# Loading one of 98 quads of a gathered edge table by single-row transfers of SyncE

## The chip, the cores and the metric

The kernel runs on one core of a Trainium2 chip. The metric is the device time of one execution in microseconds. Before the change it was 1997.35 us, the median of three runs (1996.39 to 2000.05). Five engines work side by side, each through its own list of instructions in order: TensorE (PE in the profile, PEld for its weight loads), VectorE (DVE), ScalarE (ACT), GpSimd (POOL) and SyncE (SP), which here does nothing but issue transfers. They wait for each other by semaphores.

## The reference

A layer of a graph network with attention: 12500 nodes with 128 features, 200000 edges sorted by their target, four heads of 32.

```python
h = max(layernorm(x), 0) @ W_node.T               # per node, 4 heads x 32
e = edge_attr @ W_edge.T                          # per edge
att = sum(concat(h[src], h[tgt], e) * a, -1)      # per edge and head
att = where(att > 0, att, 0.2 * att)
m = maximum(segment_max(att, tgt), 0)
ex = exp(att - m[tgt])
denom = segment_sum(ex, tgt) + (num_edges - deg) * exp(-m)
out = x + segment_sum((ex / denom[tgt]) * h[src], tgt)
```

Each edge needs the row of its source node, and the sources are in no order.

## The kernel before

A first part computes for every node a row of 137 numbers (548 bytes) and writes these rows to a table in memory. It holds the node's values h, ones, and its share of the attention as a source. A narrower table, `side`, holds the share as a target.

The edges are then worked off in **groups** of 512 places (511 edges and one place for what is carried over), four groups to a **quad**. There are 392 groups and 98 quads, numbered 0 to 97. A chunk is 128 places, so a quad has 16 chunks, and its rows fill a tile `ga` of 128 partitions by 4 groups by 4 chunks by 137 numbers. Eight such places exist: quad q lies in place q mod 8. Up to four quads make a **super**, on which a softmax is computed at once.

For each quad the following is done, by the functions named:

- `gather` (line 181) has GpSimd fetch the rows by indirect transfers, one for a chunk: 128 rows by 128 row numbers that lie in `srci`. From quad 8 on each transfer raises one of eight semaphores, and `add_sources` has ScalarE wait for the count of its quad before it copies the attention shares out of `ga` into `U` (line 735).
- `fetch`, `fetch_windows`, `fetch_inputs`, `fetch_targets` collect SyncE's loads into lists, and `issue` (line 598) puts out the next of a list: `ea`, the edge features, two in a quad; `pw`, target shares, from a row number that a register holds; `db`, the edges' places among their nodes; `inputs`, rows of x for the residual; and the results' stores to `out`. The row numbers come by register loads (line 584), one for `pw` and one for `inputs` in a quad, of as many words as the quad has windows: one up to quad 35, two up to quad 74, four behind that. `dr` (line 643), the targets for the softmax, comes once in a super.
- `all_logits` compares places on VectorE (`targets`, into `at`) and multiplies on TensorE (`logits`, into `lg`). `ea` and `pw` of quad q+2 are issued in the logits of quad q, `db` of quad q+2 at the start of the logits of quad q+1, since it has two places.
- `softmax` works on a super, and `sums` multiplies the rows of `ga` by the weights and adds them up by target on TensorE (line 1122); a division follows and the store.

The program is written out in one order, and each engine gets its instructions in it. `together` interleaves the steps of several of these functions: the sums of a quad run beside the logits of a quad some four later, one group of the one beside one of the other. `sums` ends each group with `issue("inputs", "results")`. GpSimd's list is therefore nothing but gathers, and each waits only until the place of the quad eight before it is free, that is, until TensorE has finished that quad's sums.

The tile `db` has two places of 4 x 512 words. From quad 10 on the places of edges are single bytes, so that most of the tile is free.

Of the kernel before, what the change touches and what calls it, by code (L numbers as in the profile page):

```python
# [39 lines left out]
QUADS = 8  # L40
# [6 lines left out]
SQUARE = 32  # L47
TWO = 2
HELD = 3
SETS = max(NODE_T, QG * J)  # L50
PAD = 1 << 20

# [17 lines left out]
def kernel(  # L70
# [39 lines left out]
    nc = tc.nc  # L110
    NT = -(-(N + P) // P)
    NP = NT * P
# [8 lines left out]
    table = dram.tile([NP, ROW], F32, name="table")  # L121
# [33 lines left out]
    quads = blocks(G, QG)  # L155
# [10 lines left out]
    ga_all = consts.tile([P, QUADS, QG, J, ROW], F32, name="ga")  # L166
    GA, GATHERED = {}, set()
    arrived = [tc.alloc_semaphore(f"rows{k}") for k in range(QUADS)]
    landings = {}

    def gather(q, rows, width, lo, hi):

        g0, m = quads[q]
        ga = GA[q] = ga_all[:, q % QUADS]
        chunks = lambda i: -(-min(E - (g0 + i) * NE + 1, GE) // P)
        for i in range(lo, hi):
            if chunks(i) < J:
                nc.vector.memset(ga[:, i, chunks(i):, :], 0.0)
        order = [(i, j) for i in range(lo, hi) for j in range(chunks(i))]
        for i, j in order:  # L180
            came = nc.gpsimd.indirect_dma_start(  # L181
                out=ga[:, i, j, 0:width], out_offset=None, in_=rows,
                in_offset=bass.IndirectOffsetOnAxis(ap=srci[:, g0 + i, j:j + 1], axis=0))
            if q >= QUADS:
                came.then_inc(arrived[q % len(arrived)], 16)
                tc.no_tile_sem_insts.add(came.ins.name)
                tc.add_to_no_dep_group(f"rows{q}", came.ins)
                landings[q] = landings.get(q, 0) + 16
# [27 lines left out]
    with tc.manual_schedule():  # L216
# [165 lines left out]
        def fetch_targets(q):  # L382
            g0, m = quads[q]
            n = P if class_of(q)[1] == WIDE else NARROW
            db, rows = db_all[:, q % 2], dst.rearrange("(g e) -> g e", e=GE)
            if q >= OFFSETS:
                db = db.rearrange("p g e -> p (g e)")[:, 0:QG * GE // 4].bitcast(U8)
                db, rows = db.rearrange("p (g e) -> p g e", e=GE), offset
            DB[q] = db
            return [(db[:n, lo:lo + k, :],  # L390
                     rows[g0 + lo:g0 + lo + k].unsqueeze(0).to_broadcast([n, k, GE]))
                    for lo, k in blocks(m, QG if q >= OFFSETS else PLACES_BY)]
# [150 lines left out]
    with tc.tile_pool(name="work", bufs=2) as work, \  # L543
# [91 lines left out]
        def fetch_rows(s):  # L635
            g0, m = groups(s)
            dr = DR[s] = turned.tile([SBG * H, NE + 2], I32, name="dr", bufs=2)
            if finer(s) > 1:
# [4 lines left out]
            nc.sync.dma_start(dr[0:H * m, :],  # L643
                              dst_rows[g0:g0 + m, :].unsqueeze(0).to_broadcast([H, m, NE + 2]))

        def open_logits(q):
            if q == supers[of_quad[q]][0]:
                fetch_rows(of_quad[q])
            if q + 2 < nq:
                fetch(q + 2)  # L650
            AT[q] = work.tile([P, QG, GE], BF16, name="at")
# [68 lines left out]
        def add_sources(q):  # L720

            s = of_quad[q]
            g0, m = quads[q]
            s0, sm = groups(s)
            keep_logits(q)
            if s not in U:
                U[s] = turned.tile([P, J, SBG * H], F32, name="U", bufs=2)
            f = finer(s)
            u = U[s][:, 0:J // f, 0:sm * H * f].rearrange("p c (h w) -> p w c h", h=H)[
                :, (g0 - s0) * f:(g0 - s0 + m) * f]  # L730
            if q >= QUADS:
                nc.scalar.wait_ge(arrived[q % len(arrived)],
                                  sum(landings[a] for a in range(QUADS, q + 1)
                                      if a % len(arrived) == q % len(arrived)))
            taken = nc.scalar.copy(u, GA[q][:, :m].rearrange("p g (f c) r -> p (g f) c r", f=f)[  # L735
                :, :, :, R_SRC:R_SRC + H])
            if q >= QUADS:
                tc.declare_no_dep(taken.ins, group=f"rows{q}",
                                  reason="a semaphore counts the gathers of this quad")
                tc.declare_fence(taken.ins, group=f"rows{q}")  # L740
            for kept in (EA, DB, PW, AT):
                del kept[q]
# [318 lines left out]
        def sums(q):  # L1061
# [36 lines left out]
            for i in range(m):  # L1098
# [31 lines left out]
                if not later and i == (2 if k > 1 else 1):  # L1130
                    entered()
                    if k == 1:
                        settled()
                complete(new)
                if k == 1:
                    begun.append((q, i, ga, hot, pt, acc, fc))
                if i == 2 and QUADS <= q < first_fold - 5 and of_quad[q + 1] == s:
# [735 lines left out]
```

## Time and profile before

| What | Value |
|---|---|
| median of three runs | 1997.35 us |
| the profiled execution's own time | 1993.67 us |
| its span, first to last instruction | 1991.8 us |
| busy: GpSimd / VectorE / TensorE / ScalarE | 75% / 60% / 57% / 16% of the span |
| indirect gathers on GpSimd | 1494 from the table, 72 from x |
| mean busy share of the 16 DMA engines | 0.4 to 0.5 after the first part |
| software queue (GpSimd's) / hardware queue (SyncE's) | 109.61 MB / 116.14 MB |

The page counts GpSimd's indirect transfers as busy, but not what SyncE does to issue one: an issue appears with its duration only in the timeline and in the answers on one source line, as engine SPq. There a row gives the shortest, the median and the longest duration in ns and the first and last start in us. A row of the waits names the waiting line, whom it waited for, the total in us, how often and the longest.

### The profile page before, as it was taken

How to read it: one execution, taken by the hardware profiler on the slowest of the kernel's cores; microseconds unless marked ns; L12 is line 12 of the kernel's file. 1: busy time of each engine (PE TensorE's matmuls, PEld its weight loads, DVE VectorE, ACT ScalarE, POOL GpSimd, SP SyncE). 2: the span in 40 equal slices, each digit the busy share in tenths (PEclk: the TensorE clock that was granted, in tenths of full speed). 3: DMA queues.
4: the chain of work that ended last, by engine and by line, in shares of the span. 5: the costliest groups of instructions: out<-in, count | busy, mean ns of one | idle time of the engine just before them, and what ended most of it. 6: DMA issues, size and time to landing. Idle time of an engine off the chain costs nothing. (4 is left out here: it accounts for less than half of the span.)

```text
span 1991.8 us, 18871 instructions
## 1 busy us (share of the span) xinstructions
PE 1140.5 (57%) x5116; PEld 780.2 (39%) x5116; DVE 1193.3 (60%) x2615; ACT 318.3 (16%) x1077; POOL 1491.3 (75%) x1585
## 2 busy tenths in 40 slices
PE   6566676556464655554646555546465555455565
PEld 5444454334243433342434333334343333233344
DVE  8676786456374554564746546647465474367676
ACT  6564111001011010010110100101000011122122
POOL 7777777777777777777777777777777777777774
PEclk9788788676676776767767767677777666777778
DMA  7754754434344444344444444444444444444442
GB/s 254 209 141 98 175 132 111 105 93 110 97 108 104 119 98 114 96 108 112 119 101 113 106 110 108 108 114 115 104 107 105 105 120 98 112 109 116 99 106 51
DMA packets 167748, 229.57 MB, mean 115 GB/s; under 512 B 60827, under 2 KB 100669, under 8 KB 167638
## 3 DMA queue, kind: packets, MB, share of 16 engines
q0 software_dynamic: 50112, 109.61, 24.7%
q1 hardware_dynamic: 115824, 116.14, 20.5%
q10 hardware_dynamic: 1702, 2.59, 0.4%
q8 instruction: 41, 0.67, 0.1%
q14 instruction: 69, 0.57, 0.1%
HBM read 210.74 MB, written 17.43 MB: 115 GB/s over the span
## 5 line engine op out<-in xcount | busy, mean ns | idle before, releaser
L181 POOL DMA_INDIRECT ga<-table,srci x1494 | 1413.7, 946 | 456.0 <-issue 407.9
L1122 PE MATMUL acc<-ga,hot 128*113 128x137 f32 (+1 forms) x2928 | 546.2, 346 | 81.5 <-DVE hot L1031 53.6
L1122 PEld LDWEIGHTS acc<-ga,hot 128*113 128x113 f32 (+1 forms) x2928 | 486.5, 216 | 182.2 <-issue 100.4
L956 DVE SCALAR_TENSOR_TENSOR pt<-pt,spare,acc 1x133 f32<-1x133 f32 x113 | 38.3, 339 | 523.5 <-ACT den_of L950 522.1
L691 PE MATMUL lg<-at,pw 112*96 112x512 bf16 (+2 forms) x392 | 157.2, 438 | 278.7 <-DVE at L658 265.8
L688 PE MATMUL lg<-ea,by_pair 128*96 128x512 f32 (+1 forms) x392 | 229.6, 671 | 7.1 <-ACT tg L701 7.1
L658 DVE TENSOR_TENSOR at<-const_ps,db 112x1024 bf16<-112x1024 f32 (+1 forms) x176 | 212.8, 1210 | 3.3 <-DMA db<-offset 3.3
L1089 DVE TENSOR_TENSOR ga<-ga,ex_ps 128x1056 f32<-128x1056 f32 x147 | 182.2, 1239 | 0.0
L792 PE MATMUL t_ps<-ident,U 128*64 128x128 f32 (+2 forms) x210 | 47.2, 397 | 208.9 <-ACT U L735 208.9
L735 ACT COPY U<-ga 128x64 f32<-128x64 f32 x98 | 29.0, 297 | 806.5 <-DMA ga<-table,srci 806.5
L1091 DVE TENSOR_TENSOR hot<-const_ps,slot 128x896 f32<-128x896 f32 (+1 forms) x147 | 144.1, 980 | 0.0
L792 PEld LDWEIGHTS t_ps<-ident,U 128*64 128x64 f32 (+2 forms) x210 | 37.1, 201 | 234.9 <-ACT U L735 231.6
L887 PE MATMUL ex_ps<-ident,stack 128*128 128x128 f32 x105 | 28.6, 424 | 170.2 <-DVE stack L879 157.0
L975 PEld LDWEIGHTS acc<-pt,spare 1*2 1x2 f32 x226 | 14.1, 86 | 209.0 <-issue 200.8
L691 PEld LDWEIGHTS <-pw 112*96 112x96 bf16 (+2 forms) x392 | 54.4, 139 | 102.2 <-issue 99.1
L887 PEld LDWEIGHTS ex_ps<-ident,stack 128*128 128x128 f32 x105 | 18.5, 215 | 184.3 <-ACT stack L877 184.3
L1048 DVE TENSOR_TENSOR ga<-ga,ex_ps 128x528 f32<-128x528 f32 x92 | 63.6, 693 | 38.6 <-ACT xs L893 38.5
L181 POOL DMA_INDIRECT ga<-in_x_dram,srci x72 | 68.3, 948 | 23.2 <-issue 19.2
L701 ACT COPY tg<-lg 96x512 f32<-96x512 f32 (+1 forms) x51 | 29.5, 578 | 293.8 <-PE lg L691 284.4
L920 PE MATMUL acc<-ga,hot 128*81 128x137 f32 x176 | 43.2, 334 | 52.7 <-ACT ga L928 50.8
L717 PE MATMUL t_ps<-tg,of_head 96*64 96x512 f32 (+3 forms) x96 | 72.5, 848 | 0.0
L717 PEld LDWEIGHTS t_ps<-tg,of_head 96*64 96x64 f32 (+3 forms) x96 | 12.0, 174 | 154.1 <-issue 150.9
(209 smaller groups left out, 1318.6 us busy)
## 6 DMA issues: line engine op xcount, KB each, us to landing
ea<-in_edge_t_dram SPq DMA_DIRECT2D x196, 256.0 KB
ga<-table,srci POOLq DMA_INDIRECT x1494
db<-offset SPq DMA_DIRECT2D x53, 256.0 KB
db<-in_dst_dram SPq DMA_DIRECT2D x20, 320.0 KB
db<-offset SPq DMA_DIRECT2D x35, 160.0 KB
table<-row SPq DMA_DIRECT2D x9, 616.5 KB
xt<-in_x_dram SPq DMA_DIRECT2D x9, 576.0 KB
inputs<-in_x_dram SPq DMA_DIRECT2D x92, 56.0 KB
```

Source lines behind the costliest of these rows:

```text
L181: came = nc.gpsimd.indirect_dma_start(out=ga[:, i, j, 0:width], out_offset=None, in_=rows, in_offset=bass.IndirectOffsetOnAxis(ap=srci[:, ...
L658: nc.vector.tensor_tensor(AT[q][:span, i:i + n, :].rearrange("p g e -> p (g e)"), part_ps[:span].to_broadcast([span, n * GE]), DB[q][:span ...
L688: nc.tensor.matmul(lg, by_pair[:, begin:begin + n], ea[:, i // 2, :], start=half == 0 and i == 0, stop=False, skip_group_check=True)
L691: nc.tensor.matmul(lg, PW[q][:span, begin:begin + n], at[:span, i, :], start=False, stop=full and i == quads[q][1] - 1, skip_group_check=True)
L717: nc.tensor.matmul(TP[s][:groups(s)[1] * H], of_head[supers[s][1], p][:n], tg[:n], start=p == 0, stop=False, skip_group_check=True)
L792: nc.tensor.matmul(t_ps[:R, j * P:(j + 1) * P], u[:, j, :R], ident, start=False, stop=j == C - 1, skip_group_check=True)
L887: nc.tensor.transpose(turned_ps[:, j, :], stack[:, j * P:(j + 1) * P], ident)
L920: nc.tensor.matmul(acc, hot[:, i, 0, 0:acc.shape[0]], ga[:, i, 0, :], start=False, stop=stop)
L1048: engine.tensor_tensor(val, val, weight.unsqueeze(3).to_broadcast([P, J, H, HW]), op=OP.mult)
L1089: nc.vector.tensor_tensor(val, val, weight.unsqueeze(3).to_broadcast([P, TWO * J, H, HW]), op=OP.mult)
L1091: nc.vector.tensor_tensor(hot[:, i:i + TWO, :, 1:1 + span].rearrange("p g j c -> p (g j) c"), lane_ps[:, 0:span].unsqueeze(1).to_broadcast ...
L1122: nc.tensor.matmul(acc, hot[:, i, j, 0:1 + span], ga[:, i, j, :], start=new and j == J - 1 and not second, stop=k > 1 and i % k == k - 1 a ...
```

## The change

Quad 84, the 85th, is not gathered. Its 2048 rows come by 2048 transfers of SyncE, one row of 548 bytes each, into a place of their own in the free part of the tile `db`. Each takes its row number from a register. A register load fetches 16 such numbers at a time from one partition of the same tile; they come there by a small transfer of 128 numbers for a chunk, and VectorE multiplies them by 548 to make addresses in bytes. `single_rows` is called behind each group's sums, from quad 11 on, and issues eight rows, so that 256 calls make the 2048. It asks for the numbers of the next chunk ahead, at a chunk's first call. Two semaphores count the rows, and ScalarE waits for both ahead of quad 84's copy. The bytes of `db` for quads from 10 on now lie next to each other, which leaves the room.

```diff
+SINGLE, SINGLES_FROM, AT_A_STEP = 84, 11, 8
...
     def gather(q, rows, width, lo, hi):
 
+        if q == SINGLE:
+            return
...
             if q >= OFFSETS:
-                db = db.rearrange("p g e -> p (g e)")[:, 0:QG * GE // 4].bitcast(U8)
+                at = q % 2 * QG * GE // 4
+                db = db_all.rearrange("p k g e -> p (k g e)")[:, at:at + QG * GE // 4].bitcast(U8)
...
+        def fetch_places(n):
+            if n >= QG * J:
+                return
+            g, j = quads[SINGLE][0] + n // J, n % J
+            at = ((g // 2 * J + j) * 2 + g % 2) * P
+            nc.sync.dma_start(places[n % 2], src[at:at + P].unsqueeze(0))
+
+        def scale_places(n):
+            if n < QG * J:
+                nc.vector.tensor_scalar(places[n % 2], places[n % 2], float(4 * ROW), None,
+                                        op0=OP.mult)
+
+        def single_rows():
+            if not single["step"]:
+                fetch_places(0)
+                scale_places(0)
+            n, at = divmod(single["step"], steps)
+            if n >= QG * J:
+                return
+            single["step"] += 1
+            if not at:
+                fetch_places(n + 1)
+            if at == steps // 2:
+                scale_places(n + 1)
+            lo = at * AT_A_STEP
+            if at % 2 == 0:
+                single["values"] = nc.values_load_multi_w_load_instructions(
+                    places[n % 2][:, lo:lo + 2 * AT_A_STEP], engines=[mybir.EngineType.SP],
+                    min_val=0, max_val=(NP - 1) * 4 * ROW,
+                    skip_runtime_bounds_check_because="a node's row")[1]
+            for p in range(lo, lo + AT_A_STEP):
+                came = nc.sync.dma_start(
+                    as_bytes(GA[SINGLE][p:p + 1, n // J, n % J, :]),
+                    rows_at(table, single["values"][p - at // 2 * 2 * AT_A_STEP], 4 * ROW, 1))
+                came.then_inc(single_came[2 * n // (QG * J)], 16)
+                tc.no_tile_sem_insts.add(came.ins.name)
+                tc.add_to_no_dep_group(f"rows{SINGLE}", came.ins)
+                single["landings"] += 16
...
-            if q >= QUADS:
+            if q == SINGLE:
+                assert single["landings"] == 16 * P * QG * J
+                for came in single_came:
+                    nc.scalar.wait_ge(came, single["landings"] // 2)
+            elif q >= QUADS:
...
                 complete(new)
+                if q >= SINGLES_FROM:
+                    single_rows()
```

What the change moves on SyncE is seen best in the list of its instructions for one quad, here one of those with two windows, from the store of one quad's first result on. Before (`out_dram` are the results, `base_row` and `base_side` the row numbers for `inputs` and `pw`):

```order
L598 DMA out_dram<-res 112x512
L598 DMA ea<-in_edge_t_dram 128x512
L598 DMA out_dram<-res 112x512
L584 TENSOR_LOAD base_row
L598 DMA inputs<-in_x_dram 112x512
L584 TENSOR_LOAD base_side
L598 DMA inputs<-in_x_dram 112x512
L598 DMA pw<-side 112x24
L598 DMA ea<-in_edge_t_dram 128x512
L598 DMA db<-offset 128x2048
L598 DMA pw<-side 112x24
```

And after, the same place in the program:

```order
L603 DMA out_dram<-res 112x512
L603 DMA ea<-in_edge_t_dram 128x512
L694 DMA db<-table 1x548 x8
L603 DMA out_dram<-res 112x512
L589 TENSOR_LOAD base_row
L689 TENSOR_LOAD db
L694 DMA db<-table 1x548 x8
L603 DMA inputs<-in_x_dram 112x512
L589 TENSOR_LOAD base_side
L694 DMA db<-table 1x548 x8
L603 DMA inputs<-in_x_dram 112x512
L603 DMA pw<-side 112x24
```

Then follow the second `ea`, `db` and `pw`, another register load of line 689 and another eight rows. So four times eight rows and two register loads of 16 words came between the transfers of a quad, and none of those changed its place among the others. (The lines are those of each kernel's own file.)

GpSimd's list before, from its last constant to the first instruction behind the gathers:

```order
masks.py:199 AFFINE_SELECT ident<-ident 128x128
L133 IOTA lane 128x112
L181 DMA ga<-in_x_dram,srci 128x128 x72
L181 DMA ga<-table,srci 128x137 x1494
L1048 TENSOR_TENSOR ga<-ga,xe 128x4x132 x5
```

And after:

```order
masks.py:199 AFFINE_SELECT ident<-ident 128x128
L134 IOTA lane 128x112
L185 DMA ga<-in_x_dram,srci 128x128 x72
L185 DMA ga<-table,srci 128x137 x1478
L1108 TENSOR_TENSOR ga<-ga,xe 128x4x132 x5
```

Sixteen gathers from the table are gone, and the order of the others is as it was.

More of the change, by code (lines that the diff above doesn't have):

```diff
@@ L168 @@
     arrived = [tc.alloc_semaphore(f"rows{k}") for k in range(QUADS)]
+    single_came = [tc.alloc_semaphore(f"single{k}") for k in range(2)]
     landings = {}
     def gather(q, rows, width, lo, hi):
+        if q == SINGLE:
+            return
         g0, m = quads[q]
@@ L644, in fetch_rows @@
                               dst_rows[g0:g0 + m, :].unsqueeze(0).to_broadcast([H, m, NE + 2]))
+        own = db_all.rearrange("p k g e -> p (k g e)")
+        n_own = QG * J * ROW
+        GA[SINGLE] = own[:, QG * GE // 2:QG * GE // 2 + n_own].bitcast(F32).rearrange(
+            "p (g j r) -> p g j r", g=QG, j=J)
+        places = [own[0:1, QG * GE // 2 + n_own + k * P:QG * GE // 2 + n_own + (k + 1) * P]
+                  for k in range(2)]
+        single = {"step": 0, "landings": 0}
+        steps = -(-P // AT_A_STEP)
+        def fetch_places(n):
[34 more added lines that the diff above has]
+                single["landings"] += 16
         def open_logits(q):
@@ L730, in add_sources @@
                 :, (g0 - s0) * f:(g0 - s0 + m) * f]
-            if q >= QUADS:
+            if q == SINGLE:
[3 more added lines that the diff above has]
+            elif q >= QUADS:
                 nc.scalar.wait_ge(arrived[q % len(arrived)],
-                                  sum(landings[a] for a in range(QUADS, q + 1)
-                                      if a % len(arrived) == q % len(arrived)))
+                                  sum(landings[a] for a in range(QUADS, q + 1) if a != SINGLE
+                                      and a % len(arrived) == q % len(arrived)))
             taken = nc.scalar.copy(u, GA[q][:, :m].rearrange("p g (f c) r -> p (g f) c r", f=f)[
```

## The prediction

> **What bounds the kernel now.** I began with the page's busy shares and its groups of instructions.
>
> ```profile
> span 1991.8 us, 18871 instructions
> ...
> PE 1140.5 (57%) x5116; PEld 780.2 (39%) x5116; DVE 1193.3 (60%) x2615; ACT 318.3 (16%) x1077; POOL 1491.3 (75%) x1585
> ...
> L181 POOL DMA_INDIRECT ga<-table,srci x1494 | 1413.7, 946 | 456.0 <-issue 407.9
> ...
> L956 DVE SCALAR_TENSOR_TENSOR pt<-pt,spare,acc 1x133 f32<-1x133 f32 x113 | 38.3, 339 | 523.5 <-ACT den_of L950 522.1
> ...
> L735 ACT COPY U<-ga 128x64 f32<-128x64 f32 x98 | 29.0, 297 | 806.5 <-DMA ga<-table,srci 806.5
> ```
>
> (L956 serves below.) GpSimd is the busiest engine, and almost all its idle time (407.9 of 456.0 us) is put down to "issue": it waits for nobody. ScalarE waits 806.5 us for what it gathers. The timeline of GpSimd shows the pace.
>
> ```profile
> 1001.06 0.94 POOL L181 DMA_INDIRECT ga<-table,srci  x1 [0.30 <-issue]
> 1002.30 0.94 POOL L181 DMA_INDIRECT ga<-table,srci  x1 [0.30 <-issue]
> ...
> 1701.08 0.94 POOL L181 DMA_INDIRECT ga<-table,srci  x1 [0.30 <-issue]
> ...
> 1961.75 0.94 POOL L181 DMA_INDIRECT ga<-table,srci  x1 [0.30 <-issue]
> ```
>
> One gather starts every 1.25 us, so a quad of 16 takes 20.0 us, from the first table rows to the last gather at 1961.75; the other engines follow. SyncE, which the change loads, is off that path: for its transfers it stands waiting for results. Its waits and its instructions between 311 and 1591 us (the stretch that matters below):
>
> ```profile
> SPq L598 <- DVE res L1333: 841.0, 64, 17.2
> ...
> L598 SPq DMA_DIRECT2D ea<-in_edge_t_dram x129: 357/422/1346, 311.0 to 1590.2; - x129
> L598 SPq DMA_DIRECT2D pw<-side x123: 317/338/1341, 316.1 to 1589.8; - x123
> L598 SPq DMA_DIRECT2D inputs<-in_x_dram x106: 317/322/569, 311.8 to 1590.8; - x106
> L598 SPq DMA_DIRECT2D out_dram<-res x100: 334/345/361, 330.9 to 1589.3; - x100
> L598 SPq DMA_DIRECT2D db<-offset x64: 349/369/1438, 317.0 to 1574.2; - x64
> L643 SPq DMA_DIRECT2D dr<-in_dst_rows_dram x16: 594/624/635, 369.3 to 1570.7; - x16
> ```
>
> The three numbers are the shortest, median and longest time in ns for which SyncE itself is held by one instruction: issuing is not free.
>
> **What is taken away.** 16 gathers of quad 84, 16 x 1.25 = 20.0 us of GpSimd. If nothing else became late, the span would be 1991.8 - 20.0 = 1971.8 us.
>
> **What SyncE gets.** 2048 loads of one row, 128 register loads of 16 words, 16 loads of row numbers. They stand eight behind each group from quad 11 to quad 74, so in 64 quads: 32 rows and two register loads in each. By the order on SyncE the first eight come just ahead of the first of these transfers, the last ones just ahead of the second:
>
> ```profile
> 311.80 0.33 SPq L598 DMA_DIRECT2D inputs<-in_x_dram  x1
> ...
> 1590.75 0.36 SPq L598 DMA_DIRECT2D inputs<-in_x_dram  x1
> ```
>
> 1279 us for 64 quads, 20.0 each. What does SyncE need for one quad when it never waits? First its present work: by the counts and medians above 129 x 0.422 + 123 x 0.338 + 106 x 0.322 + 100 x 0.345 + 64 x 0.369 + 16 x 0.624 = 198 us. Then its register loads, one word each up to quad 35, two words after that, four words from quad 75:
>
> ```profile
> L584 SPq TENSOR_LOAD <-base_row x14: 264/269/291, 428.4 to 688.1; - x14
> ...
> L584 SPq TENSOR_LOAD <-base_row x35: 469/475/576, 811.5 to 1489.4; - x35
> ...
> L584 SPq TENSOR_LOAD <-base_row x13: 863/884/1009, 1670.3 to 1893.9; - x13
> ```
>
> Two in a quad: 24 x 2 x 0.27 + 40 x 2 x 0.475 = 51 us. Between two issues lie a register move and the sequencer's gaps:
>
> ```profile
> 1574.64 0.36 SPq L598 DMA_DIRECT2D pw<-side  x1
> 1575.10 0.37 SPq L598 DMA_DIRECT2D inputs<-in_x_dram  x1
> ```
>
> 0.46 from start to start, 0.36 of it the issue: 0.10 us around each, for some 666 of them 66 us. Together 315 us, 4.9 in a quad; for the long ones (up to 1438 ns) I take 5.1.
>
> **The register load of 16 words** is not in this trace. 0.269, 0.475 and 0.884 us for one, two and four words are a straight line: 0.206 and then 0.204 a word. Carried on, 0.884 + 12 x 0.2045 = 3.34 us, 3.43 with its gap, 6.86 in a quad. From below it costs what four words cost, 0.88 (1.9 in a quad, with gaps). I take the line, since three points lie on it.
>
> Two pages of the Trainium skill disagree here. Runtime: NRT & Kernel Launch, section "Instruction fetch mechanics", gives some 200 ns a register even in bulk: the trace's 205 ns a word agrees, and it would make the same 3.3 us. DMA: Bandwidth & Descriptors, section "Latency and other measured facts", has a floor of about 600 ns that one spreads by loading several at once; 269 ns for one word lies below it, and by it 16 words would cost little more than four. What the kernel does then is the first rival.
>
> **A load of one row** is not there either: all transfers of SyncE have 80 rows or more. The nearest rows are ScalarE's, which issues a few of one row and one of eight (the 300 of the third line):
>
> ```profile
> L1493 ACTq DMA_DIRECT2D rows<-in_dst_ends_dram x1: 245/245/245, 425.8 to 425.8; - x1
> L1170 ACTq DMA_DIRECT2D rows<-in_fine_ends_dram x1: 266/266/266, 1795.5 to 1795.5; - x1
> L1517 ACTq DMA_DIRECT2D rows<-in_dst_rows_dram x4: 300/334/339, 605.6 to 765.5; - x4
> L402 ACTq DMA_DIRECT2D ends_i<-in_dst_ends_dram x1: 728/728/728, 5.6 to 5.6; - x1
> ```
>
> The last stands in the start-up, where its neighbours are long too; I leave it to a rival. So an issue of one row holds SyncE for 0.245 us at least and 0.34 (as for 80 rows and more) at most. An address from a register does not raise it: pw has one and costs 0.338, ea has none and costs 0.422. But inputs costs 0.32 behind other work and 0.37 right behind another issue (the pair above), and seven rows of eight stand right behind another. I take 0.265, near the one-row lines: 0.365 with move and gaps, 32 x 0.365 = 11.7 us in a quad. The row numbers add 16 x 0.45 / 64 = 0.1, and VectorE 16 multiplications of one row, some 0.3 us each (339 ns for the one-row form quoted first), hidden in its 40% of idle time. The bytes are those that the gathers moved.
>
> **The sum.** 5.1 + 11.7 + 6.9 + 0.1 = 23.8 us of SyncE in a quad, against 20.0 of GpSimd. SyncE becomes the bound for 64 quads. Its instructions are in order, so ea, pw, db and inputs of later quads queue behind the rows, and TensorE and VectorE wait for these: db, the shortest lead, is issued at the start of one quad's logits for the next quad. That lead lets the others run at most one quad ahead; it takes up the first lag and no more. GpSimd can't run on alone either: quad q+8 is gathered where quad q lay, so it stops at most eight quads ahead of the sums and idles some 3.8 us in a quad. Row by row: SyncE puts out its last row at 311.8 + 64 x 23.8 = 1835 us instead of 1591. At that point the sums are in quad 75 or 76, and gather 85, the next but one since 84 is left out, needs the place of quad 77: one or two quads more at the others' own pace. That pace is 12.1 us of VectorE in a quad:
>
> ```profile
> 1601.00:1900.00 299.00, 166.32 (x734) 113.63 (x734) 181.78 (x338) 56.36 (x239) 226.44 (x239) 0.73 0.45 111
> ```
>
> (us, then busy time of PE, PEld, DVE, ACT, POOL; 181.78 of VectorE in 15 quads.) I allow 25 us. From gather 85 on, GpSimd has what it had before: 1991.8 - 1701.1 = 291 us to the end. The others have some 20 quads to go in it at 13 to 14 us, enough. The new span is 1835 + 25 + 291 = 2151 us. The skipped gathers are in it already, and they buy little: GpSimd waited anyhow.
>
> The profiled execution took 1993.67 us, 1.9 over its span, and lies 3.7 under the median of the runs, 1997.35. So 2151 + 1.9 + 3.7 = 2157, rounded to **2155 us**, 7.9% slower. One ns on the row costs 2048 ns: at 0.245 the time is 2114, at 0.34 it is 2309. If the others need 50 us instead of 25, it is 25 more.
>
> **Rivals.**
>
> *SyncE keeps up.* The register load is the pivot. Without the line SyncE fits: 5.1 + 11.7 + 1.9 + 0.1 = 18.8 us, under 20.0, and then only the 16 gathers count: 1997.35 - 20.0 = 1977 us, faster. By the sum SyncE stays hidden while 32 rows and two register loads cost under 14.8 us a quad, against 18.6 as I price them. For it speaks that SyncE idles 841 us today; against it, three points on one line. 8%.
>
> *SyncE just over the edge.* The row's move and gaps overlap the issue, so that a row costs 0.30 from start to start: 5.1 + 9.6 + 6.9 + 0.1 = 21.7 us, and 627 + 64 x 21.7 + 5.6 = 2021 us (627 being 311.8 + 25 + 291). Against it: the gaps stand at every issue of the trace. 5%, with the few times within 0.2%.
>
> *The row is dearer than 80 rows.* At 0.42, like ea, a quad takes 28.7 us and the kernel 627 + 1837 + 6 = 2470; at 0.728, like the one-row load of the start-up, 38.6 us and 3103. This comes if the queue holds SyncE up when transfers follow so closely; the long issues of 1.2 to 1.4 us in the trace stand single. 7%.
>
> *The change does not bring the rows in time.* ScalarE waits for all 2048 ahead of quad 84's logits. They are out five quads before, at least 60 us; they land in a few. I give no chance of its own.
>
> **How the numbers follow.** The forecast has 80%. Its own range is that of the row, 2114 to 2309. The range of 8 in 10 goes from 2070 (half the way to the edge case) to 2310 and leaves out the first rival, most of the second and the third. This kernel's measurement can tell about 0.2% from no change. Faster 8%, the first rival; within 0.2% 2%; slower 90%.
>
> **What would show it.** In the new profile: 2048 issues of table rows on SyncE with a median of 245 to 300 ns; 128 register loads of about 3.34 us; SyncE's wait for res far under 841 us between the first and the last row, with that stretch some 1520 us long instead of 1279; GpSimd's 16 gathers 24 us apart there with waits for TensorE (a place not free), and 1.25 us from gather to gather after it; ScalarE's wait for gathers mostly gone, new waits of TensorE and VectorE for ea, pw, db and inputs. If the stretch stays at 1279 us, the register loads or the rows were overpriced and the first rival holds. If it is longer but SyncE still waits for results in it, my bound is the wrong one.

## The result, and the profile after

| | before | after |
|---|---|---|
| median (range) | 1997.61 us (1996.39 to 2000.05) | 1977.07 us (1976.45 to 1979.86) |
| ratio (95% interval) | | 0.9902 (0.989 to 0.9914) |
| span of the profiled execution | 1991.8 us | 1974.6 us |

The change made the kernel 1.0% faster. The forecast was 2155 us, 7.9% slower; what came was its first rival, "SyncE keeps up", to the microsecond: 1977. It had been given 8%.

In three sets of runs late in the study the kernel before took 2403 to 2426 us, a fifth longer, and the changed one 9 to 10% more than that; the cause is not known, and what was measured there decides nothing.

The page of the changed kernel, those rows that answer to the ones shown of before:

```profile
span 1974.6 us, 23134 instructions
...
PE 1134.7 (57%) x5116; PEld 776.4 (39%) x5116; DVE 1196.4 (61%) x2631; ACT 318.3 (16%) x1077; POOL 1478.0 (75%) x1569
...
L185 POOL DMA_INDIRECT ga<-table,srci x1478 | 1400.1, 947 | 451.7 <-issue 414.4
...
L714 DVE TENSOR_TENSOR at<-const_ps,db 112x1024 bf16<-112x1024 f32 (+1 forms) x176 | 212.9, 1210 | 41.8 <-DMA db<-offset 41.7
...
L795 ACT COPY U<-ga 128x64 f32<-128x64 f32 x97 | 28.7, 297 | 787.4 <-DMA ga<-table,srci 787.3
```

GpSimd still waits for nobody, and ScalarE still waits for the gathers, 787 us instead of 806. The one new wait among these rows is that of L714 for `db`, 42 us in all; the forecast had it as the wait by which SyncE's lag spreads, and it stayed small. The timeline of GpSimd at the end of the stretch in which SyncE loads rows:

```profile
1599.51 0.94 POOL L185 DMA_INDIRECT ga<-table,srci  x1 [0.30 <-issue]
1600.76 0.94 POOL L185 DMA_INDIRECT ga<-table,srci  x1 [0.30 <-issue]
1602.00 0.95 POOL L185 DMA_INDIRECT ga<-table,srci  x1 [0.30 <-issue]
```

The pace is the old one, 1.25 us from gather to gather, and 16 gathers are missing: 16 x 1.25 = 20.0 us, against 20.5 between the medians. What SyncE needs for its additions, by the answers on the two lines that issue them (shortest, median and longest in ns):

```profile
L689 SPq TENSOR_LOAD <-db x128: 971/1167/1203, 326.8 to 1593.4; - x128
...
L694 SPq DMA_DIRECT2D db<-table x2048: 224/228/333, 328.1 to 1601.5; - x187
```

A register load of 16 words took 1.17 us where 3.34 had been priced. A row held SyncE for 0.228 us where 0.265 had been priced. The stretch is 1273 us long, 19.9 a quad: the rows are put out at GpSimd's pace, not at SyncE's. This was the sign that the prediction named for its first rival (a stretch that stays at 1279 us). SyncE still waits for results there, 52 us instead of 841 (its waits from 311 to 1610 us):

```profile
SPq L603 <- DVE res L1395: 52.3, 27, 7.4
```

That fall was named as a sign of the forecast bound, and it came without the bound: it shows only that SyncE has more to do.

Eight rows follow each other so, by the timeline of SyncE:

```profile
1039.84 2.56 SPq L694 DMA_DIRECT2D db<-table  x8
1042.50 0.32 SPq L603 DMA_DIRECT2D inputs<-in_x_dram  x1
1043.65 2.52 SPq L694 DMA_DIRECT2D db<-table  x8
```

2.56 us for eight, 0.32 from start to start. The present register loads changed too:

```profile
L589 SPq TENSOR_LOAD <-base_side x14: 461/474/796, 428.8 to 687.7; - x14
L589 SPq TENSOR_LOAD <-base_row x13: 442/540/687, 441.3 to 682.5; - x13
...
L589 SPq TENSOR_LOAD <-base_row x36: 662/684/800, 801.3 to 1498.4; - x36
L589 SPq TENSOR_LOAD <-base_side x35: 662/668/1073, 807.3 to 1482.9; - x35
```

Those of one word had been 0.27 us and those of two 0.475; each is 0.2 us longer. The prediction's sum, made again with these rows and the other transfers as they were: 198 + 24 x 1.01 + 40 x 1.35 + 66 = 342 us, 5.4 in a quad; 32 x 0.32 = 10.2; 2 x (1.17 + 0.09) = 2.5; 0.1 for the row numbers. That is 18.2 us of SyncE in a quad, under GpSimd's 20.0. By the sum SyncE has 1.8 us left of the 15 that it had; its waits between the first and the last row add up to 100 us, which is 1.6 in a quad.

### The profile page after: what moved, and what is told of

The parts are those of the page before. It is cut to its first block, busy times and chain, and to the rows that moved or that the text cites. A ratio compares the mean times of both kernels' runs of the same rounds, so it can differ in the third digit from the quotient of the medians.

```text
span 1974.6 us, 23134 instructions
## 1 busy us (share of the span) xinstructions
PE 1134.7 (57%) x5116; PEld 776.4 (39%) x5116; DVE 1196.4 (61%) x2631; ACT 318.3 (16%) x1077; POOL 1478.0 (75%) x1569
## 3 DMA queue, kind: packets, MB, share of 16 engines
q1 hardware_dynamic: 119952, 117.28, 20.8%
## 4 chain that ended last, share of the span: by engine, by line
POOL 30%; DVE 27%; PE 15%; issue 13%; DMA 8%; ACT 5%; SPq 1%; ACTq 0%; POOLq 0%; DVEq 0%
POOL ga L185 30%; DMA ga<-table,srci 6%; PE acc L1182 6%; DVE at L714 4%; PE t_ps L852 2%; PE lg L744 2%; PE lg L747 1%; DVE t_ps L866 1%; DVE t_ps L865 1%; DVE t_ps L932 1%; DVE ga L1108 1%; DVE pt L1016 1%; DVE t_ps L929 1%; DVE ga L1149 1%; DVE stats L289 1%
## 5 line engine op out<-in xcount | busy, mean ns | idle before, releaser
L714 DVE TENSOR_TENSOR at<-const_ps,db 112x1024 bf16<-112x1024 f32 (+1 forms) x176 | 212.9, 1210 | 41.8 <-DMA db<-offset 41.7
L185 POOL DMA_INDIRECT ga<-in_x_dram,srci x72 | 68.6, 952 | 23.3 <-issue 18.3
L744 PEld LDWEIGHTS lg<-ea,by_pair 128*96 128x96 f32 (+1 forms) x392 | 63.5, 187 | 13.1 <-ACT tg L757 8.6
```

What stands on the lines that cost most here:

```text
L185: came = nc.gpsimd.indirect_dma_start(out=ga[:, i, j, 0:width], out_offset=None, in_=rows, in_offset=bass.IndirectOffsetOnAxis(ap=srci[:, ...
L714: nc.vector.tensor_tensor(AT[q][:span, i:i + n, :].rearrange("p g e -> p (g e)"), part_ps[:span].to_broadcast([span, n * GE]), DB[q][:span ...
L744: nc.tensor.matmul(lg, by_pair[:, begin:begin + n], ea[:, i // 2, :], start=half == 0 and i == 0, stop=False, skip_group_check=True)
```

## The experiments

The theory after the result: the bound was right (SyncE's instructions in order, at a sum per quad, with 20.0 us as the edge), and one price was wrong, that of the load of 16 words. The rival: SyncE is no bound at all, since others wait for its transfers with more slack than was thought, and any price would have been hidden.

**What a register load costs.** The three points of the prediction were loads from lists whose words begin wherever a quad's windows do. The first experiment puts loads of known place and length into the kernel before, one behind each group's sums, and behind each a transfer of one row. Nothing is left out.

```diff
+            if k == 2:
+                at = words(**load_words(0, 4))[1]
+            if k == 3:
+                at = words(**load_words(2, 4))[1]
...
+            if k == 6:
+                at = words(**load_words(0, 16))[1]
+            if k == 7:
+                at = words(**load_words(1, 16))[1]
+            nc.sync.dma_start(as_bytes(trial), rows_at(table, at[-1], 4 * ROW, 1))
```

(`load_words(lo, n)` takes n words from the word `lo` of a list that begins at a multiple of 64 bytes, counted, as everywhere below, from the begin of its tile.)

> The kernel before, all gathers kept, with one extra register load on SyncE behind each group of quads 11 to 74 and one row of the table loaded by its last word, to nowhere in use. Eight shapes in turn, 32 of each: 1, 2, 4 and 8 words from a multiple of 64 bytes, 4 and 8 words from 8 bytes behind it, 16 words from the multiple, 16 words from 4 bytes behind it. The straight line of the prediction (0.205 us a word): 0.27, 0.47, 0.88, 0.88, 1.70, 1.70, 3.34, 3.34 us. Rival one, a load works in pieces of four aligned words, one price of 0.2 us for each piece: 0.27, 0.27 to 0.47, 0.27, 0.47 to 0.88, 0.47, 0.68 to 1.7, 0.88 to 1.0, 1.1 to 3.3. Rival two, the price stops growing with the count at some four words, wherever they lie: 0.27, 0.47, 0.88, 0.88, 0.9 to 1.1 for all the others, and no difference between the two places. Time: SyncE has some 1.3 us more in 20 us, so no change by any theory, 1994 to 2001 us.

The answers on the lines of this kernel, in the order 1, 2, 4 words at the list's begin, 4 from its third word, 8 at its begin, 8 from its third word, 16 at its begin, 16 from its second word:

```profile
L664 SPq TENSOR_LOAD <-db x32: 276/283/297, 325.1 to 1556.2; - x32
L666 SPq TENSOR_LOAD <-db x32: 468/473/481, 326.7 to 1558.5; - x32
L668 SPq TENSOR_LOAD <-db x32: 478/502/515, 329.1 to 1561.8; - x32
L670 SPq TENSOR_LOAD <-db x32: 1060/1068/1084, 331.6 to 1569.7; - x32
L672 SPq TENSOR_LOAD <-db x32: 532/538/553, 333.7 to 1573.3; - x32
L674 SPq TENSOR_LOAD <-db x32: 1667/1674/1687, 335.7 to 1576.9; - x32
L676 SPq TENSOR_LOAD <-db x32: 1150/1182/1205, 339.3 to 1581.4; - x32
L678 SPq TENSOR_LOAD <-db x32: 3457/3472/3502, 349.3 to 1592.3; - x32
```

The same 16 words cost 1.18 us from the list's begin and 3.47 us from four bytes further. Off the begin the price runs at some 0.2 us a word, as the prediction's line did (3.34 forecast, 3.47 measured); at the begin, eight words cost hardly more than two.

One word and two cost at the list's begin what they cost the kernel before (0.28 and 0.47). It is the third point of the prediction's line that lies badly: the kernel's own four-word loads begin eight bytes behind a multiple of 16 and took 0.88 us, where four words at the list's begin take 0.50. (In the ladder four such words took 1.07; why more than 0.88 is open.) The changed kernel takes its 16 words at multiples of 64 bytes.

None of the three theories fits whole: the line misses the aligned loads, the pieces of four words are nearest but would have had four at 0.27 and 16 at 1.0 at most, and the third foresaw no difference between the two places. In its one run the kernel took 1995.75 us beside 1995.19 of before, no difference.

**The predicted price, put back.** One edit to the changed kernel: the lists lie one word further, so that every load of 16 words is one of the slow ones.

```diff
-        places = [own[0:1, QG * GE // 2 + n_own + k * P:QG * GE // 2 + n_own + (k + 1) * P]
+        places = [own[0:1, QG * GE // 2 + n_own + 1 + k * P:QG * GE // 2 + n_own + 1 + (k + 1) * P]
```

> The change with one edit: the lists of row numbers lie four bytes further, so that none of the loads of 16 words begins at a multiple of 64 bytes. In the ladder such a load held SyncE for 3.47 us, about what the prediction had priced (3.34), and an aligned one for 1.18. Theory (the predicted bound was right, and only the load was mispriced): two loads cost some 4.8 us more in a quad, SyncE needs 21.9 us in quads up to 35 and 24.0 behind them instead of 17.1 and 19.2; its last row goes out at about 328 + 25 x 21.9 + 39 x 24.0 = 1811 us, and with the 25 and 291 us of the prediction the span is 2127 us, between 2100 and 2160. SyncE's wait for results is gone in the stretch, and GpSimd's gathers stand further apart than 1.25 us there. Rival (SyncE is no bound, its waits give way whatever it has to do): under 1985 us. The register loads of one and two words, which were some 0.2 us longer in the changed kernel than before: the same in this one by either.

2136.9 us (2134.81 to 2141.55), 1.0692 of before (1.0674 to 1.071): the forecast's 2155 within 1%. Its load and rows, VectorE's waits and GpSimd's, and GpSimd's timeline where the last row goes out:

```profile
L689 SPq TENSOR_LOAD <-db x128: 3268/3465/3543, 324.3 to 1808.1; - x128
...
L694 SPq DMA_DIRECT2D db<-table x2048: 224/228/389, 327.9 to 1818.5; - x187
```

```profile
DVE at L714 <- DMA db<-offset: 717.9, 68, 16.2
```

```profile
POOL ga L185 <- PE acc L1182: 148.6, 50, 7.7
```

```profile
1797.78 0.94 POOL L185 DMA_INDIRECT ga<-table,srci  x1 [0.30 <-issue]
1822.74 0.94 POOL L185 DMA_INDIRECT ga<-table,srci  x1 [24.02 <-PE acc L980]
1823.99 0.94 POOL L185 DMA_INDIRECT ga<-table,srci  x1 [0.31 <-issue]
```

What the prediction foresaw is here in the main. VectorE waits for `db`, 718 us; SyncE never waits for a result between 311 and 1820 us; GpSimd stops for a place that is not free, for 24 us just as the last row goes out, and then runs on at 1.25 us. The last row goes out at 1818 us (1835 forecast), and from it to the end pass 2133.8 - 1818.5 = 315 us (25 + 291 = 316 forecast). The row stretch is 23.3 us long per quad (23.8 forecast). The rival falls: SyncE does become a bound.

That the time is so near the forecast is in part luck. By these rows the sum is 5.4 + 10.2 + 2 x (3.47 + 0.09) + 0.1 = 22.8 us, and 34 us of short waits in the stretch make the 23.3: the row was priced 1.5 us a quad too high, and the waits, the present work, the load and a stretch that begins 16 us later made up for most of it.

And GpSimd is not held up from the start. Its waits for TensorE from 700 to 1000 us, and then from 1000 to 1300 us:

```profile
POOL ga L185 <- PE acc L1182: 3.0, 3, 2.4
```

```profile
POOL ga L185 <- PE acc L1182: 50.6, 13, 7.7
```

So the first lag of SyncE goes into the lead that GpSimd has over the sums; the next experiment shows how much.

**A price in between.** The changed kernel with eight loads of four words in a quad instead of two of 16; each begins at a multiple of 16 bytes.

```diff
-            if at % 2 == 0:
-                single["values"] = nc.values_load_multi_w_load_instructions(
-                    places[n % 2][:, lo:lo + 2 * AT_A_STEP], engines=[mybir.EngineType.SP],
...
+                if p % 4 == 0:
+                    single["values"] = nc.values_load_multi_w_load_instructions(
+                        places[n % 2][:, p:p + 4], engines=[mybir.EngineType.SP],
```

> The changed kernel with eight register loads of 4 aligned words in a quad in the place of two of 16. This is meant to make SyncE as dear as the prediction had it. Theory: SyncE becomes the bound where its work in a quad passes 20 us, and the time is then 627 us plus its work in 64 quads (the prediction's formula). If 4 aligned words cost 0.87 to 1.07 us, SyncE needs some 23.2 us in a quad up to 35 and 25.4 after it, and the kernel takes some 2200 us (2170 to 2240). If they cost 0.27 to 0.47 us (pieces of four words), SyncE stands at 18.5 and 20.6 us and the time is 1975 to 2010. Rival: SyncE's queue does not bound the kernel, whatever it has to do, and the time stays at 1977 us also with loads of 0.87 us.

1989.99 us (1989.51 to 1991.53), 0.9972 of before (0.996 to 0.9985).

```profile
L690 SPq TENSOR_LOAD <-db x512: 297/536/743, 325.7 to 1672.3; - x171
```

```profile
DVE at L714 <- DMA db<-offset: 477.9, 61, 14.9
```

8 x (0.54 + 0.1) = 5.1 us of loads instead of 2.5 give a sum of 20.8 us, 0.8 over GpSimd's pace, and the kernel loses 14 of the 20 us (spans of 1989.1 and 1974.6). The stretch of rows is 21.0 us per quad; 13 us of waits in it make the difference to the sum. The prediction's formula began the stretch at 311.8 us; in these kernels the first row goes out 14 to 16 us later, since SyncE has to wait once for the first list to be multiplied:

```profile
SPq L690 <- DVE db L671: 12.8, 1, 12.8
```

From there 326 + 64 x 21.0 + 316 = 1986 us, against a span of 1989.1. GpSimd stops for a place once only, as SyncE puts out its last rows (its waits from 311 to 1700 us):

```profile
POOL ga L185 <- PE acc L980: 14.3, 1, 14.3
```

From the last row to the end pass 373 us in the changed kernel (1974.6 - 1601.5) and 315 in this one and the one before it. Up to that difference, 58 us, SyncE may fall behind without costing anything, since GpSimd has gathered ahead. Over 64 quads that is 0.9 us in each: the stretch lengthens from 20.0 us on, the kernel only from some 20.8.

**Where the gain comes from.** Two kernels part the change's two halves. In the first the rows are loaded by SyncE beside `db`, but quad 84 is gathered as well, and its own gathers are used. In the second quad 84 is neither gathered nor loaded: its place is set to zero once, so that this quad's sources are left out of the result.

```diff
-        if q == SINGLE:
-            return
...
-        GA[SINGLE] = own[:, QG * GE // 2:QG * GE // 2 + n_own].bitcast(F32).rearrange(
+        beside_db = own[:, QG * GE // 2:QG * GE // 2 + n_own].bitcast(F32).rearrange(
```

```diff
-                if q >= SINGLES_FROM:
-                    single_rows()
+                if q == SINGLES_FROM and not i:
+                    nc.vector.memset(GA[SINGLE], 0.0)
```

> The changed kernel with quad 84 gathered as before; the 2048 single rows are loaded into their place too, but only waited for and not used. It tells what SyncE's rows cost by themselves. If they are hidden, as the result suggests: as before, 1997 us, ratio 0.998 to 1.002. If they cost something that the skipped gathers pay back: slower than before by it, 2000 to 2010 us.

> The changed kernel without the single rows: quad 84 is neither gathered nor loaded, its place is set to zero once, so the sums of its edges are left out. It tells what 16 gathers are worth with nothing in their place: by the pace of GpSimd 16 x 1.25 = 20 us, so 1977 us, ratio to before 0.990 as the change itself. If the single rows cost something, it is faster than the change by that: 1970 us or less.

With both it took 1994.58 us, 0.9998 of before (0.9988 to 1.0007): 2048 rows and 128 register loads cost nothing that can be measured. With neither it took 1974.59 us, 0.989 (0.9873 to 0.9906): the 16 gathers are worth 20.6 us. The change's 0.9902 holds nearly all of it.

**Another engine.** The changed kernel with ScalarE in SyncE's place, for the rows and their register loads alike; beside it the changed kernel itself, on the same chip.

```diff
-                    places[n % 2][:, lo:lo + 2 * AT_A_STEP], engines=[mybir.EngineType.SP],
+                    places[n % 2][:, lo:lo + 2 * AT_A_STEP], engines=[mybir.EngineType.Activation],
...
-                came = nc.sync.dma_start(
+                came = nc.scalar.dma_start(
```

> The change with one edit: ScalarE issues the 2048 rows and loads the registers, at the same places of the program, and SyncE does only what it did before. Theory (an issue is hidden on any engine that has 12.5 us to spare in a quad; ScalarE works 318 us, 3.3 in a quad, and 1.1 for each register load): 1977 us as for the change, within 3. Rival (ScalarE's rows delay its copies): over 1985 us. For the register loads of one and two words on SyncE: if the rows ahead of them made them 0.2 us longer in the changed kernel, they are back at 0.27 and 0.475 us here; if it was the place of the numbers in the memory, they stay at about 0.5 and 0.67.

> The changed kernel itself, beside the others of this call: 1977 us by any theory, 0.990 of the kernel before.

1980.97 us (1980.46 to 1981.47), 0.9905 of before (0.9888 to 0.9921), and 1979.2 for the changed kernel, 0.9896 (0.9879 to 0.9912). ScalarE hides the rows as well. The issue of a row on it, and then its waits, which show what is pushed back and does not matter:

```profile
L694 ACTq DMA_DIRECT2D db<-table x2048: 227/235/809, 328.0 to 1598.5; - x187
```

```profile
ACT U L795 <- DMA ga<-table,srci: 490.2, 52, 15.9
ACT tg L757 <- issue: 195.7, 30, 7.2
ACT hot L1080 <- issue: 185.6, 48, 4.2
```

It waits some 300 us less for gathers than in the changed kernel, and stands 381 us ahead of the copies of lines 757 and 1080 without a wait that the profile shows, which is where its rows are issued. SyncE's own register loads answer the second question of this run only in part:

```profile
L589 SPq TENSOR_LOAD <-base_row x14: 266/272/352, 430.0 to 690.4; - x14
L589 SPq TENSOR_LOAD <-base_side x14: 262/452/984, 430.7 to 691.9; - x14
...
L589 SPq TENSOR_LOAD <-base_row x35: 467/475/576, 816.4 to 1494.0; - x35
L589 SPq TENSOR_LOAD <-base_side x35: 465/667/1405, 817.3 to 1495.7; - x35
```

Those of `base_row` are back at 0.27 and 0.475 us; those of `base_side` are mixed, and why is open. The kernel with neither rows nor gathers settles the place of the numbers, which lie there as in the changed one:

```profile
L589 SPq TENSOR_LOAD <-base_side x14: 265/270/925, 429.9 to 690.5; - x14
...
L589 SPq TENSOR_LOAD <-base_side x35: 465/473/1372, 813.3 to 1492.1; - x35
```

So it is the work added to SyncE that made them longer, and by these two kernels not its amount: in the ladder, with one load and one row behind a group, they took 0.48 to 0.50 and 0.67 to 0.68 us too.

**Two quads.** With SyncE nearly full and ScalarE free, a second quad can be had: behind each group's sums SyncE issues eight rows and ScalarE eight, first for quad 49 (in the sums of quads 12 to 43), then for quad 90 in the same place (quads 52 to 83).

```diff
+SINGLES, SINGLES_FROM, AT_A_STEP = (49, 90), (11, 51), 8
...
+        issuers = [(nc.sync, mybir.EngineType.SP), (nc.scalar, mybir.EngineType.Activation)]
...
+            for half, (queue, engine) in enumerate(issuers):
+                base = (at // 2 * 2 + half) * 2 * AT_A_STEP
...
+                for v in range(at % 2 * AT_A_STEP, (at % 2 + 1) * AT_A_STEP):
+                    p = base + v
+                    came = queue.dma_start(
```

> Two quads, 49 and 90, are not gathered, one after the other in the same free place: behind each group's sums SyncE loads eight rows and ScalarE eight, from quad 12 to 43 for the one and from 52 to 83 for the other, and the first list of row numbers is asked for four groups ahead of its use. Theory (SyncE has room for 32 rows and two register loads in a quad, and ScalarE too): 32 gathers less than before, 2 x 20.6 = 41 us, so about 1955 us, 20 us under the change. Rival (ScalarE's copies, for which VectorE and TensorE wait, come late behind its rows): the gathers saved are given back, 1975 us or more; then the waits for den_of, for xs and for stack have grown.

1975.67 us (1970.47 to 1978.38), 0.9884 (0.9867 to 0.99): not to be told from the change, though 16 more gathers are gone and the last gather starts 20.7 us earlier than in the changed kernel beside it (1925.5 against 1946.2 us). VectorE's waits from 1500 to 1800 us, in this kernel and then in the changed one:

```profile
DVE at L722 <- DMA db<-offset: 85.8, 11, 14.8
```

```profile
DVE at L714 <- DMA db<-offset: 4.1, 3, 2.2
```

It is `db` again, that is, SyncE, whose own waits for results from 1500 to 1700 us are gone, 37 us of them in the changed kernel: from quad 75 on a quad has four windows, so SyncE has more transfers and longer register loads of its own. ScalarE's late copies were the other suspect; but from 1500 to 1800 us VectorE's wait for `den_of` from ScalarE fell from 43.7 to 20.5 us. To tell them apart by the time, the rows were kept out of the quads of four windows: quad 48 whole and three groups of quad 80, in the sums of quads 12 to 43 and 51 to 74, with the last group of quad 80 gathered. Against it stood two whole quads that lie a little earlier, 48 and 87.

```diff
-SINGLES, SINGLES_FROM, AT_A_STEP = (49, 90), (11, 51), 8
+SINGLES, SINGLES_FROM, AT_A_STEP, LOADED = (48, 80), (11, 50), 8, (4, 3)
...
+        if q in SINGLES:
+            ga, lo = GA[q], max(lo, LOADED[SINGLES.index(q)])
```

> The kernel with two quads that are not gathered, with the quads 48 and 87 instead of 49 and 90, so that the second list of rows stands behind the sums of quads 51 to 82. In the run with 49 and 90 VectorE waited 85 us for the places of edges (db) from 1500 to 1800 us, where a quad has four windows and SyncE more transfers of its own, and the last 10 quads were then worked off late. Theory (SyncE is the bound there, as it was for the prediction's 23.8 us, and the gathers saved are given back to it): the overlap with the quads of four windows is still eight quads, so these waits for db stay, at 50 us or more, and the time stays between 1960 and 1975 us. Rival (only the last quads were too few to catch up): 1958 us or less, with waits for db as before.

> Quad 48 is not gathered at all, and of quad 80 only the last group is: its other three are loaded as rows, by SyncE and ScalarE together, behind the sums of quads 51 to 74, that is, before the quads of four windows begin. 28 gathers fewer than before, 16 of them the change's. Theory (SyncE and ScalarE both have room up to quad 74, and gathers saved there are kept): 28 x 1.25 = 35 us less than before, about 15 us less than the change: 0.9825 of before, 1962 to 1967 us, and VectorE's waits for db under 50 us. Rival (ScalarE's rows delay its copies): 1975 us or more.

> The changed kernel itself, beside the two others: 0.990 of the kernel before.

The same three kernels were run twice more:

> The kernel with quad 48 and three quarters of quad 80 loaded as rows by SyncE and ScalarE, once more, since in the run before it everything on the chip was slower, the kernel before too (2403 us). Theory (SyncE and ScalarE both have room up to quad 74, and gathers saved there are kept): 28 x 1.25 = 35 us less than before, 0.9825 of it, 1962 to 1967 us, and VectorE's waits for db under 50 us. Rival (ScalarE's rows delay its copies): 1975 us or more.

> The kernel with quads 48 and 87 loaded as rows, once more for the same reason. Theory (SyncE is the bound in the quads of four windows): VectorE's waits for db between 1500 and 1800 us stay at 50 us or more and the time between 1960 and 1975 us. Rival (only the last quads were too few to catch up): 1958 us or less.

> The changed kernel itself, beside the two others: 0.990 of the kernel before.

> The kernel with quad 48 and three quarters of quad 80 loaded as rows, on a chip where the kernel before takes about 2000 us. Theory (SyncE and ScalarE both have room up to quad 74, and gathers saved there are kept): 0.9825 of the kernel before, 15 us under the change, and VectorE's waits for db under 50 us. Rival (ScalarE's rows delay its copies): 0.9875 or more. If the kernel before takes 2400 us as in the last two calls, the change is at 1.09 and this kernel at 1.14, as there, since SyncE's instructions are stretched and SyncE is the bound.

> The changed kernel itself: 0.990 where the kernel before takes about 2000 us; 1.09 where it takes 2400.

> The kernel with quads 48 and 87 loaded as rows. Theory (SyncE is the bound in the quads of four windows): VectorE's waits for db between 1500 and 1800 us stay at 50 us or more and the time at 0.98 to 0.9875 of the kernel before. Rival (only the last quads were too few to catch up): 0.979 or less.

In these three sets the kernel before took 2403, 2426 and 2405 us, the changed one 1.097, 1.0921 and 1.0908 of it, the quad and three quarters 1.1404, 1.1478 and 1.134, and the two quads 1.1635, 1.1736 and 1.1612. The forecasts for a kernel before of some 2000 us missed there; what the third set foresaw for such a case, 1.09 and 1.14, was read off the two before it. These sets leave the question open.

At the kernel's usual time the quad and three quarters ran once more, at 1994.57 us for before.

> The kernel with quad 48 and three quarters of quad 80 loaded as rows, for the last time. Theory (SyncE and ScalarE both have room up to quad 74, and gathers saved there are kept): where the kernel before takes about 2000 us, 0.9825 of it, 35 us less, and VectorE's waits for db under 50 us. Rival (ScalarE's rows delay its copies): 0.9875 or more. Where the kernel before takes 2400 us, 1.14 as in the earlier calls.

1962.17 us (1961.11 to 1962.38), 0.9836 (0.9822 to 0.9849): 32 us under before, where 28 gathers are 35, and better than the change, with the intervals apart. VectorE's and ScalarE's waits, the first of 1500 to 1800 us, the others of the whole run:

```profile
DVE at L723 <- DMA db<-offset: 11.0, 4, 4.6
```

```profile
ACT tg L766 <- issue: 183.7, 28, 10.6
ACT hot L1090 <- issue: 161.9, 42, 4.3
```

ScalarE's copies are pushed back as in the run with ScalarE alone, and at most 3 us are lost; the waits for `db` are small, and the gain stays. That makes SyncE in the quads of four windows the likely taker of the 20 us of the two quads. It is not shown alone, since quad 80 also lies further from the end than quad 90, and the kernel that would part these two, with 48 and 87, has no measurement at the usual time.

## Why the prediction was wrong

- *What bounds the kernel now*: right. GpSimd sets the time, 1.25 us a gather, and the 16 gathers are worth what was said (20.0 forecast, 20.6 measured with the quad left out).
- *The register load of 16 words*: this is the step that failed. "Three points on a line" was a line in the number of words; that the third came from words that begin eight bytes behind a multiple of 16, and the loads to be priced begin at multiples of 64 bytes, was not asked. At the price of 3.34 us SyncE's sum was 23.8 us; at the 1.17 measured this term falls from 6.9 us to 2.5, and with it alone the sum is 19.4, under the edge; with the row alone put right it would still be 22.3. The bound from below (0.88, as four words) was much nearer. Of the two pages of the Trainium skill set against each other, Runtime: NRT & Kernel Launch, "Instruction fetch mechanics", with its 200 ns a register, agrees with the loads that lie badly (3.47 us for 16), and not with those at a multiple of 64 bytes (1.18); the page speaks of loads from HBM, and these come from a tile.
- *A load of one row*: too dear, 0.365 us against 0.32 from start to start. 0.228 us of issue is under the lower bound of 0.245, the cheapest one-row transfer that the trace had. In a quad it is 1.5 us.
- *SyncE's present work*: too cheap by 0.3 us in a quad (5.1 against 5.4), since SyncE's old register loads grow longer among the added work. That a new neighbour changes the price of an old instruction was not in the sum, nor was SyncE's one wait of 12.8 us for the first list.
- *The sum and the edge*: the mechanism was right. At the predicted price the kernel took 2137 us, with the wait for `db`, the place not free and the 315 us behind the last row as forecast, though the nearness of the total is in part luck. With SyncE's own waits in the stretch the sums close in all three kernels: 18.2 + 1.6 = 19.8 (19.9 measured), 20.8 + 0.2 = 21.0 (21.0), 22.8 + 0.5 = 23.3 (23.3). The edge was put too low: 20.0 us, or 14.8 for the additions, is where the stretch begins to lengthen; the time begins to grow at some 20.8. The prediction's own formula says so (627 + 64 x 21.0 = 1971, the span with the gathers gone), but its text had GpSimd idle 3.8 us in every quad, without the lead.
- *The rivals*: the first one named the pivot, the load off the line, and its time. Its 18.8 us a quad against 18.2 are partly luck, with the load and the present work too cheap and the row too dear; the time would have been the same at 18 or 19. Its chance of 8% was too small for a price that no row of the trace showed, with the two bounds at 0.88 and 3.34 us, and the range of 2070 to 2310 left it out altogether. The rows dearer than 80 rows did not come; the rows were in time.

## What to carry to other kernels

A price read off a trace belongs to the kind of instruction that was measured there, and a line through three sizes says nothing of what was not varied by itself, here the place where the words begin; where the forecast turns on such a price and its two bounds lie on different sides of the edge, the chances have to go by the bounds, not by the fit. Look where lists that are loaded into registers begin: here a shift of one word off the multiples of 64 bytes cost 158 us (2136.9 against 1979.2). An engine that only issues transfers can carry work for a crowded one, but count its time per stage of the program, the stage with the most transfers first, since its lateness returns through the shortest lead, here that of `db`, once the crowded engine's own lead, here 58 us, is used up.

## What was not expected of the hardware

- A register load's time depends on where its words begin: 0.54 us for eight words at a multiple of 64 bytes and 1.67 eight bytes further, 1.18 and 3.47 us for 16. Which multiple is enough was not tried for 16; four words at multiples of 16 bytes took 0.536.
- Register loads of SyncE took 0.2 us longer once other loads and single rows stood between them (0.27 to 0.47 and 0.54, 0.475 to 0.67 and 0.68), as much with one load and one row behind a group as with eight rows. With the rows on ScalarE half of them were back, with no rows at all every one.
- An issue of one 548-byte row from a register's address held SyncE for 0.228 us and ScalarE for 0.235, less than one of 80 rows and more (0.32 to 0.42).
